# Two column tiles per transfer to the transposed adjacency, and list blocks of 128 columns instead of 124

## The chip, the cores and the metric

One core of a Trainium2 chip runs the whole kernel. The metric is device time in microseconds. The median of three runs before the change is 1015.22 us (1012.13 to 1015.25).

## What is computed

Four graph layers in sequence over 2708 nodes with 128 features each, in float32. `adj` is a 2708 x 2708 matrix, about 0.6% nonzero beside its diagonal; its pattern of nonzeros is symmetric, its values are not.

```python
def _L0_gnn_ref(X, H):                      # layer 0
    msg = jnp.matmul(H.T, X)
    inv_deg = 1.0 / H.sum(axis=0)
    inv_deg = jnp.where(jnp.isinf(inv_deg), 0.0, inv_deg)
    return msg * inv_deg[:, None]
...
messages = gelu(s[:, None, :] + d[None, :, :] + msg_b)     # layer 1, per nonzero
aggregated = jnp.einsum('ijd,ij->id', messages, adj)
...
agg = adj @ states                                         # layer 2, then a GRU cell
...
e = jnp.where(mask, leaky_relu(s_src[:, None] + s_dst[None, :]), NEG)   # layer 3, two heads
att = softmax(e, axis=1) @ h + x
```

Each layer starts with `h = max(layernorm(x), 0)` and ends with `x = x + layer(h, adj)`.

## The kernel before

Rows and columns are cut in tiles of 128 (`P`): 21 whole tiles and one of 20. Four tiles make a group, so there are six groups of rows (`s`) and six of columns (`c`); the last has two tiles, of 128 and 20.

**Layer 0** is a walk over cuts of `adj`: column group `c` outside, row group `s` inside (`order`, line 544). For each cut (`c`, `s`) it does four things at once.
- SyncE loads the cut, 512 columns and some more, into one of five buffers (`load_cut`, line 310, issue at line 320; `RING = 5`, line 286). The load of a cut two steps ahead is written in the program ahead of the step's own work (line 570). Cuts of the last column group (`z`) have buffers of their own and are loaded during the chunk `LAST - 2`, one a step (line 572).
- VectorE makes lists: for every row it takes the eight largest values of each block of `JB` columns and their places (`list_cut`, line 348: MAX8 at 360, the index search at 362). There are `NB` = 22 blocks. The blocks that hold the diagonal ("near" blocks) are first copied and cleared of it by GpSimd (`mask_near`, line 328: copy at 342, product at 343).
- TensorE turns the cut, tile by tile (transposes, line 406, into three buffers of PSUM), and multiplies it with `h` (line 392).
- ScalarE copies each turned column tile out of PSUM into a buffer `aT`, summing the degrees on the way (line 411), and sends it to `adjT` in HBM (`write_one`, line 366, issue at line 368). Layer 2 reads `adjT` much later (line 1388). One turn handles one column tile of four row tiles, 128 x 512 values or 256 KB; `aT` has six buffers. A write is issued one turn after its copy, so the ScalarE queue holds: copy, write of the turn before, one or two small steps of the layer norms (`next_steps`, `first_steps`), next copy.

All queues run in the order in which the program is written; `invert` (line 431) puts the first use of the summed degrees of a column group on VectorE, two steps into the next group (one step in the last).

The list blocks are `JB` = 124 wide, the tiles 128, so a cut must hold four list blocks and four tiles: its window (line 306) begins at 496 c and ends at 512 (c + 1), that is 512, 528, 544, 560 and 576 columns wide, and 228 for the last. Every row tile has two near blocks, the last tile one.

**Lists of the last rows.** Row tiles 17 to 20 (`LATER`) have their other blocks loaded and listed during layer 1, five a period (`late_blocks`, line 199; `load_late`, line 708; `list_late`, line 732); there are 80 of them. The last tile's are done by `load_wide` and `list_wide`.

**Layer 1** takes the listed entries per block (at most 128 of a block of 128 rows), gathers both ends with selection matrices, applies gelu and scatters. Its matrices per block have `width(b)` rows, up to `JB` (line 936). If a block holds more than 128 entries, or a row has eight in one block, a flag is set and a dense version of the whole computation runs (`check_lists`, line 1036).

The tile framework gives out the DMA semaphores: in the trace only eight numbers occur (101 to 108), which the DMAs of SyncE and ScalarE take in turn, in the order of the program.

Of the kernel before, what the change touches and what calls it, by code (L numbers as in the profile page):

```python
# [20 lines left out]
F32 = mybir.dt.float32  # L21
BF16 = mybir.dt.bfloat16
AF = mybir.ActivationFunctionType
ALU = mybir.AluOpType
# [6 lines left out]
P = 128  # L31
N = 2708
D = 128
NT = (N + P - 1) // P
FULL = N // P
TAIL = N - FULL * P
CH = 512
# [3 lines left out]
MASKED = -1e30  # L41
FMAX = 3.4028234663852886e38

JB = 124
NB = (N + JB - 1) // JB
S = 8
E = P
GROUPS = [(t, min(4, NT - t)) for t in range(0, NT, 4)]
# [3 lines left out]
def size(t):  # L52
    return min(P, N - t * P)


def width(b):
    return min(JB, N - b * JB)


@with_exitstack  # L60
def listed_layers(ctx: ExitStack, tc: tile.TileContext, x, adj, w, out, flag):
    nc = tc.nc
# [12 lines left out]
    adjT = dram.tile([P, NT, N], F32, name="adjT")  # L75
# [86 lines left out]
    degs = keep.tile([P, NT, len(GROUPS)], F32, name="degs")  # L162
# [27 lines left out]
    LATER = NT - 5  # L190
    AT_ONCE = 5
    EARLY = 2
    WIDE = 4

    def near_blocks(n):

        return range(n * P // JB, (n * P + size(n) - 1) // JB + 1)

    late_blocks = [(n, b) for n in range(LATER, NT - 1) for b in range(NB) if b not in near_blocks(n)]
    nc.gpsimd.memset(val[:, NT - 1, :, :], 0.0)  # L200
    nc.gpsimd.memset(col[:, NT - 1, :, :], 0.0)

# [82 lines left out]

    RING = 5
    BEHIND = 2
    WINDOW = CH + 16 * (len(GROUPS) - 2)
    l0, ending = ExitStack(), ExitStack()
    ordered = ExitStack()  # L290
    lastp = ending.enter_context(tc.tile_pool(name="l0z", bufs=1, side="right"))
# [1 line left out]
    once0 = l0.enter_context(tc.tile_pool(name="l0h", bufs=1))  # L293
    pool = l0.enter_context(tc.tile_pool(name="l0k", bufs=2))
    marked = l0.enter_context(tc.tile_pool(name="l0n", bufs=8))
    turned = l0.enter_context(tc.tile_pool(name="l0t", bufs=6))
    sump = l0.enter_context(tc.tile_pool(name="l0p", bufs=3, space=PSUM))
    turnp = l0.enter_context(tc.tile_pool(name="l0q", bufs=3, space=PSUM))
    h0 = once0.tile([P, NT, D], F32, name="h0")
# [5 lines left out]

    def window(c):

        return 4 * JB * c, min(CH * (c + 1), N)

    def load_cut(c, s):  # L310

        g0, gk = GROUPS[s]
        lo, hi = window(c)
        if c < LAST:
            a = rows_a.tile([P, 4, WINDOW], F32, name="a")
        else:
            a = lastp.tile([P, gk, hi - lo], F32, name=f"z{s}")
        cuts[c, s] = a
        if gk == 4 and (c, s) != (0, 0):
            nc.sync.dma_start(  # L320
                a[:, :, 0 : hi - lo], adj[g0 * P : (g0 + 4) * P, lo:hi].rearrange("(t p) e -> p t e", p=P)
            )
            return
        for n in range(g0, g0 + gk):
            m = size(n)
            nc.sync.dma_start(a[0:m, n - g0, 0 : hi - lo], adj[n * P : n * P + m, lo:hi])

    def mask_near(c, s):

        g0, gk = GROUPS[s]  # L330
        lo = window(c)[0]
        a = cuts[c, s]
        for n in range(g0, g0 + gk):
            m = size(n)
            for b in near_blocks(n):
                if b // 4 != c:
                    continue
                e, k = b * JB, width(b)
                e0, e1 = max(n * P, e), min(n * P + m, e + k)
                p = lastp if c == LAST else marked  # L340
                v = nears[n, b] = p.tile([P, JB], F32, name=f"near{n}_{b}" if c == LAST else "near")
                nc.gpsimd.tensor_copy(v[0:m, 0:k], a[0:m, n - g0, e - lo : e - lo + k])
                nc.gpsimd.tensor_tensor(
                    v[0:m, e0 - e : e1 - e], a[0:m, n - g0, e0 - lo : e1 - lo],
                    offdiag[0:m, e0 - n * P : e1 - n * P], ALU.mult,
                )

    def list_cut(c, s, n):

        m = size(n)  # L350
        lo = window(c)[0]
        units = []
        for b in range(4 * c, min(4 * c + 4, NB)):
            if b in near_blocks(n):
                units.append((b, nears.pop((n, b))[0:m, 0 : width(b)]))
            elif n < LATER:
                units.insert(0, (b, cuts[c, s][0:m, n - GROUPS[s][0], b * JB - lo : b * JB - lo + width(b)]))
        for k in range(0, len(units), 2):
            for b, v in units[k : k + 2]:
                nc.vector.max(val[0:m, n, b, :], v)  # L360
            for b, v in units[k : k + 2]:
                nc.vector.max_index(col[0:m, n, b, :], val[0:m, n, b, :], v)  # L362
# [7 lines left out]
    def work_cut(c, s, between=()):  # L370

        steps = iter(between)

        g0, gk = GROUPS[s]
        t0, tk = GROUPS[c]
        i0, iw = span(g0, gk)
        lo = window(c)[0]
        a = cuts[c, s]
        if s == 0:
            accs[c] = sump.tile([P, CH], F32, name="sums")  # L380

        dgs = []
        if c == s:
            for q in range(gk):
                m = size(g0 + q)
                e = (g0 + q) * P - lo
                dgs.append(marked.tile([P, P], F32, name="dg", bufs=4))
                nc.gpsimd.tensor_tensor(dgs[q][0:m, 0:m], a[0:m, q, e : e + m], ident[0:m, 0:m], ALU.mult)

        def products(n):  # L390
            m, w = size(n), span(t0, tk)[1]
            nc.tensor.matmul(  # L392
                accs[c][:, 0:w], h0[0:m, n, :], a[0:m, n - g0, t0 * P - lo : t0 * P - lo + w],
                start=(n == 0), stop=(n == NT - 1),
            )

        todo = list(range(g0, g0 + gk))
        js = list(range(t0, t0 + tk))
        turns = [js[q : q + 2] for q in range(0, tk, 2)] if gk < 4 == tk else [[j] for j in js]
        for js in turns:  # L400
            p = turnp.tile([P, CH], F32, name="p_T")
            k, n = size(js[0]), len(js)
            for i, j in enumerate(js):
                for q in range(gk):
                    m, e = size(g0 + q), j * P - lo
                    nc.tensor.transpose(  # L406
                        p[0:k, i * iw + q * P : i * iw + q * P + m], a[0:m, q, e : e + k], ident[0:m, 0:m]
                    )
            aT = turned.tile([P, CH], F32, name="aT")
            for i, j in enumerate(js):  # L410
                nc.scalar.activation(  # L411
                    aT[0:k, i * iw : (i + 1) * iw], p[0:k, i * iw : (i + 1) * iw], AF.Copy, accum_out=degs[0:k, j, s : s + 1]
                )
            write_one()
            written.append((
                adjT[0:k, js[0] : js[0] + n, i0 : i0 + iw], aT[0:k, 0 : n * iw].rearrange("p (j i) -> p j i", j=n)
            ))
            for _ in range(2 if c == 0 else 1):
                next(steps, None)
            if c > 0 and todo and gk == 4:  # L420
                products(todo.pop(0))
        for _ in steps:
            pass
        for n in todo:
            products(n)

        for q, dg in enumerate(dgs):
            m = size(g0 + q)
            nc.scalar.activation(dg[0:m, 0:m], dg[0:m, 0:m], AF.Copy, accum_out=own[0:m, g0 + q : g0 + q + 1])
# [1600 lines left out]
```

## Time and profile before

| | us |
|---|---|
| median of three runs | 1015.22 |
| the profiled execution | 1009.63 |
| its span, first to last instruction | 1007.8 |
| TensorE / VectorE / ScalarE / GpSimd busy in the span | 912.5 / 795.9 / 530.3 / 461.4 |
| layer 0, to TensorE's last product of it | 0 to 205.8 |
| lists closed, layer 1 begins | 206 to 250 |
| layer 1, then layers 2 and 3 | 250 on |
| `adjT` writes: 122, of which 105 of 256 KB | |
| loads of cuts: 24 whole groups (1024 to 1152 KB), some smaller | |
| late list loads in layer 1 | 21 |

All times below are from the profiled execution. A row of the waits says which engine and line stood idle, what released it, how long in total, how often, and the longest. A row of the windows gives, for a stretch, each engine's busy time and number of instructions, then the granted TensorE clock, the busy share of the DMA engines and the rate. A row of the timeline gives start, duration, engine, line and operation, and in brackets the idle time ahead of it and its releaser; "ACTq" and "SPq" are the issues of transfers from ScalarE's and SyncE's queues.

### The profile page before, as it was taken

The page shows a single profiled execution, that of the slowest core. Times are in us where ns is not written, and L with a number is a line of the kernel's source. Part 1 is how long each engine was busy: PE and PEld are TensorE (multiplying, and loading weights), DVE is VectorE, ACT ScalarE, POOL GpSimd, SP SyncE. Part 2 cuts the span into 40 slices and gives each one's busy share as a digit, 9 for nine tenths or more (in the row PEclk, how much of TensorE's full clock was granted, in tenths as well). Part 3 has the DMA queues.
Part 4 walks back from the last instruction along what each step waited for, and adds up shares of the span by engine and source line. Part 5 has one row for each costly group of instructions (what it writes and reads, how often), then busy time and mean ns, then how long its engine had stood idle before and what let it go on. Part 6 is the DMA issues. An engine that isn't in the chain of part 4 may idle for free. (4 is left out here: it accounts for less than half of the span.)

```text
span 1007.8 us, 22141 instructions
## 1 busy us (share of the span) xinstructions
PE 912.5 (91%) x7948; PEld 742.8 (74%) x7948; DVE 795.9 (79%) x2753; ACT 530.3 (53%) x1561; POOL 461.4 (46%) x588
## 2 busy tenths in 40 slices
PE   6799889945999999999999999999889999999983
PEld 3455455624999999999899744444678999999972
DVE  7999896976787898989966555676588977997793
ACT  5756557734666667667666324332322653564342
POOL 6413222424996779797966354443211300430142
PEclk9999999955999999999999899999899999999996
DMA  9999999422344334333322356654301574456000
GB/s 329 287 340 333 340 368 327 167 70 88 124 160 152 109 111 142 112 128 116 125 84 93 122 204 216 235 190 159 105 22 56 173 250 139 158 176 218 6 17 15
DMA packets 80458, 165.41 MB, mean 164 GB/s; under 512 B 9760, under 2 KB 25748, under 8 KB 80338
## 3 DMA queue, kind: packets, MB, share of 16 engines
q1 hardware_dynamic: 60358, 131.77, 39.7%
q10 hardware_dynamic: 19980, 32.14, 8.8%
q8 instruction: 64, 1.05, 0.4%
q14 instruction: 56, 0.46, 0.1%
HBM read 117.26 MB, written 30.87 MB: 147 GB/s over the span
## 5 line engine op out<-in xcount | busy, mean ns | idle before, releaser
L843 POOL TENSOR_SCALAR put<-count,line,value 128x128 f32<-128x128 f32 x176 | 199.7, 1146 | 10.9 <-PE agg L956 7.0
L1239 PE MATMUL att<-hv,wt 128*128 128x129 f32 x1672 | 196.0, 278 | 7.6 <-DVE wt L1209 6.2
L1239 PEld LDWEIGHTS att<-hv,wt 128*128 128x128 f32 x1672 | 192.2, 194 | 10.7 <-DVE wt L1209 8.7
L931 PE MATMUL p_m<-s,sel 128*128 128x128 bf16 x1452 | 162.3, 220 | 6.9 <-ACT g L943 4.6
L935 PE MATMUL p_m<-d,cols 124*128 124x128 bf16 (+1 forms) x1452 | 162.3, 220 | 3.9 <-DVE cols L874 3.9
L1209 DVE SCALAR_TENSOR_TENSOR wt<-row,lift,mask 128x1024 f32<-128x1024 f32 (+1 forms) x132 | 138.8, 1082 | 22.9 <-PE att L1239 22.9
L121 POOL TENSOR_TENSOR n_r<-n_r,minus_half 128x4 f32<-128x4 f32 (+1 forms) x28 | 39.6, 1413 | 243.5 <-DVE n_r L120 238.4
L956 PE MATMUL agg<-put,g 128*128 128x128 f32 (+1 forms) x968 | 123.5, 280 | 0.0
L392 PE MATMUL sums<-a,h 128*128 128x512 f32 x220 | 115.8, 622 | 1.6 <-ACT h L137 1.6
L956 PEld LDWEIGHTS agg<-put,g 128*128 128x128 f32 x968 | 114.2, 193 | 0.0
L406 PEld LDWEIGHTS p_T<-ident,a 128*128 128x128 f32 (+1 forms) x440 | 54.7, 144 | 77.1 <-issue 34.7
L931 PEld LDWEIGHTS <-sel 128*128 128x128 bf16 x1452 | 103.8, 98 | 8.6 <-issue 7.9
L1400 PE MATMUL p_agg<-a,hs 128*128 128x512 f32 (+2 forms) x264 | 107.7, 549 | 2.1 <-DMA a<-adjT 2.1
L935 PEld LDWEIGHTS <-cols 124*128 124x128 bf16 (+1 forms) x1452 | 102.8, 98 | 4.9 <-DVE cols L874 4.9
L943 ACT ACTIVATE g<-p_m 128x512 f32<-128x512 f32 x132 | 72.8, 553 | 59.4 <-PE agg L956 42.8
L852 ACT ACTIVATE put<-mine,value 128x128 f32<-128x128 bf16 x308 | 100.8, 393 | 0.0
L406 PE MATMUL p_T<-ident,a 128*128 128x128 f32 (+1 forms) x440 | 71.3, 283 | 24.6 <-ACT aT L411 18.0
L411 ACT ACTIVATE aT<-p_T 128x512 f32<-128x512 f32 (+2 forms) x132 | 71.0, 541 | 27.0 <-PE p_T L406 10.8
L1400 PEld LDWEIGHTS p_agg<-a,hs 128*128 128x128 f32 (+1 forms) x264 | 47.1, 191 | 49.2 <-issue 45.5
L362 DVE FIND_INDEX8 col<-val,a 128x8 uint16<-128x124 f32 x306 | 82.4, 281 | 0.0
L1362 ACT ACTIVATE hs<-hs 128x1354 f32<-128x1354 f32 (+1 forms) x44 | 58.4, 1329 | 39.5 <-DMA hs<-in_adj 39.1
L360 DVE MAX8 val<-a 128x8 f32<-128x124 f32 x306 | 70.9, 273 | 2.2 <-DMA a<-in_adj 2.2
(291 smaller groups left out, 1561.0 us busy)
## 6 DMA issues: line engine op xcount, KB each, us to landing
hs<-in_adj SPq DMA_DIRECT2D x42, 677.0 KB
adjT<-aT ACTq DMA_DIRECT2D x105, 256.0 KB
a<-adjT SPq DMA_DIRECT2D x20, 1280.0 KB
spread<-passed SPq DMA_DIRECT2D x22, 704.0 KB
later<-sel SPq DMA_DIRECT2D x22, 616.0 KB
a<-in_adj SPq DMA_DIRECT2D x5, 1152.0 KB
a<-in_adj SPq DMA_DIRECT2D x5, 1120.0 KB
a<-in_adj SPq DMA_DIRECT2D x5, 1088.0 KB
```

The lines of the kernel that those rows point to most:

```text
L362: nc.vector.max_index(col[0:m, n, b, :], val[0:m, n, b, :], v)
L392: nc.tensor.matmul(accs[c][:, 0:w], h0[0:m, n, :], a[0:m, n - g0, t0 * P - lo : t0 * P - lo + w], start=(n == 0), stop=(n == NT - 1),)
L406: nc.tensor.transpose(p[0:k, i * iw + q * P : i * iw + q * P + m], a[0:m, q, e : e + k], ident[0:m, 0:m])
L843: nc.gpsimd.tensor_scalar(st["put", 0][:, b, :], count, st["line"][:, b : b + 1], st["value"][:, b : b + 1], ALU.is_equal, ALU.mult,)
L852: nc.scalar.activation(st["put", 1][:, b - HP, :], st["mine"][:, b - HP, :], AF.Identity, scale=st["value"][:, b : b + 1])
L931: nc.tensor.matmul(p[:, b - b0, :], st["sel"][:, b, :], s3[:, q, t % 2, :], start=(q == 0), stop=False)
L935: nc.tensor.matmul(p[:, b - b0, :], st["cols"][0:kb, b, :], d3[0:kb, b, q, :], start=False, stop=(q == 2))
L943: nc.scalar.activation(g[:, 0:n, :], state[t].pop(("p", k))[:, 0:n, :], AF.Gelu)
L956: nc.tensor.matmul(agg, g[:, b - 4 * k, :], put, start=(b == 0), stop=False)
L1209: nc.vector.scalar_tensor_tensor(wt[:, 0:n], row[:, k, c : c + n], lift[:, j, k : k + 1], mask[:, j, c : c + n], op0=ALU.max, op1=ALU.mult,)
L1239: nc.tensor.matmul(banks[s // 3][:, s % 3, :], wt[:, q * P : (q + 1) * P], hv[:, j, k, :], start=(v < 2 and s // 3 not in touched), stop=( ...
L1400: nc.tensor.matmul(pa[:, 0:n], h[0:k, j, :], a[0:k, j - j0, 0:n], start=(j == 0), stop=(j == NT - 1))
```

## The change

List blocks become 128 wide (`JB = P`): still 22, of which the last is 20 wide instead of 104. Each row tile has one near block, exactly its diagonal tile, which GpSimd makes with one product instead of two copies and two products. The windows become 512 c to 512 (c + 1) with nothing extra, 148 for the last. Of the 84 blocks of row tiles 17 to 20 that aren't near, the first four (tile 17, blocks 0 to 3) are listed with cut (0, 4), so that 80 are left for layer 1. Column tiles go to `adjT` in pairs: `aT` has five buffers of twice the size, two turns fill one, and one transfer of 512 KB takes both. Where the row group is the last (148 rows), four column tiles go in one transfer; the last column group's tiles go one by one as before.

```diff
-JB = 124
+JB = P
...
-    late_blocks = [(n, b) for n in range(LATER, NT - 1) for b in range(NB) if b not in near_blocks(n)]
+    late_blocks = [(n, b) for n in range(LATER, NT - 1) for b in range(NB) if b != n]
+    late_blocks = late_blocks[len(late_blocks) % AT_ONCE :]
...
-    turned = l0.enter_context(tc.tile_pool(name="l0t", bufs=6))
+    turned = l0.enter_context(tc.tile_pool(name="l0t", bufs=5))
...
     def window(c):
-        return 4 * JB * c, min(CH * (c + 1), N)
+        return CH * c, min(CH * (c + 1), N)
...
-            a = rows_a.tile([P, 4, WINDOW], F32, name="a")
+            a = rows_a.tile([P, 4, CH], F32, name="a")
...
-        for n in range(g0, g0 + gk):
+        for n in range(g0, g0 + gk if c == s else g0):
             m = size(n)
-            for b in near_blocks(n):
...
-                nc.gpsimd.tensor_copy(v[0:m, 0:k], a[0:m, n - g0, e - lo : e - lo + k])
-                nc.gpsimd.tensor_tensor(
-                    v[0:m, e0 - e : e1 - e], a[0:m, n - g0, e0 - lo : e1 - lo],
-                    offdiag[0:m, e0 - n * P : e1 - n * P], ALU.mult,
-                )
+            p = lastp if c == LAST else marked
+            v = nears[n] = p.tile([P, JB], F32, name=f"near{n}" if c == LAST else "near")
+            nc.gpsimd.tensor_tensor(
+                v[0:m, 0:m], a[0:m, n - g0, n * P - lo : n * P - lo + m], offdiag[0:m, 0:m], ALU.mult
+            )
...
-            elif n < LATER:
+            elif (n, b) not in late_blocks and n < NT - 1:
...
-            aT = turned.tile([P, CH], F32, name="aT")
+            if not held:
+                aT = turned.tile([P, 2 * CH], F32, name="aT")
             for i, j in enumerate(js):
+                at = (len(held) + i) * iw
                 nc.scalar.activation(
-                    aT[0:k, i * iw : (i + 1) * iw], p[0:k, i * iw : (i + 1) * iw], AF.Copy, accum_out=degs[0:k, j, s : s + 1]
+                    aT[0:k, at : at + iw], p[0:k, i * iw : (i + 1) * iw], AF.Copy, accum_out=degs[0:k, j, s : s + 1]
                 )
             write_one()
-            written.append((
-                adjT[0:k, js[0] : js[0] + n, i0 : i0 + iw], aT[0:k, 0 : n * iw].rearrange("p (j i) -> p j i", j=n)
-            ))
+            held += js
+            if k < P or size(js[-1] + 1) < P or (len(held) + n) * iw > 2 * CH or js[-1] == t0 + tk - 1:
+                j, n = held[0], len(held)
+                written.append((
+                    adjT[0:k, j : j + n, i0 : i0 + iw], aT[0:k, 0 : n * iw].rearrange("p (j i) -> p j i", j=n)
+                ))
+                held = []
```

More of the change, by code (lines that the diff above doesn't have):

```diff
@@ L193, in listed_layers @@
     WIDE = 4
-    def near_blocks(n):
-        return range(n * P // JB, (n * P + size(n) - 1) // JB + 1)
-    late_blocks = [(n, b) for n in range(LATER, NT - 1) for b in range(NB) if b not in near_blocks(n)]
+    late_blocks = [(n, b) for n in range(LATER, NT - 1) for b in range(NB) if b != n]
+    late_blocks = late_blocks[len(late_blocks) % AT_ONCE :]
     nc.gpsimd.memset(val[:, NT - 1, :, :], 0.0)
@@ L287, in listed_layers @@
     BEHIND = 2
-    WINDOW = CH + 16 * (len(GROUPS) - 2)
     l0, ending = ExitStack(), ExitStack()
@@ L332, in mask_near @@
         a = cuts[c, s]
-        for n in range(g0, g0 + gk):
+        for n in range(g0, g0 + gk if c == s else g0):
             m = size(n)
-            for b in near_blocks(n):
[L336 to L341, printed above, removed]
-                nc.gpsimd.tensor_copy(v[0:m, 0:k], a[0:m, n - g0, e - lo : e - lo + k])
-                nc.gpsimd.tensor_tensor(
-                    v[0:m, e0 - e : e1 - e], a[0:m, n - g0, e0 - lo : e1 - lo],
-                    offdiag[0:m, e0 - n * P : e1 - n * P], ALU.mult,
-                )
+            p = lastp if c == LAST else marked
[3 more added lines that the diff above has]
+            )
     def list_cut(c, s, n):
@@ L353, in list_cut @@
         for b in range(4 * c, min(4 * c + 4, NB)):
-            if b in near_blocks(n):
-                units.append((b, nears.pop((n, b))[0:m, 0 : width(b)]))
-            elif n < LATER:
+            if b == n:
+                units.append((b, nears.pop(n)[0:m, 0:m]))
+            elif (n, b) not in late_blocks and n < NT - 1:
                 units.insert(0, (b, cuts[c, s][0:m, n - GROUPS[s][0], b * JB - lo : b * JB - lo + width(b)]))
@@ L408, in work_cut @@
                     )
-            aT = turned.tile([P, CH], F32, name="aT")
+            if not held:
+                aT = turned.tile([P, 2 * CH], F32, name="aT")
             for i, j in enumerate(js):
+                at = (len(held) + i) * iw
                 nc.scalar.activation(
-                    aT[0:k, i * iw : (i + 1) * iw], p[0:k, i * iw : (i + 1) * iw], AF.Copy, accum_out=degs[0:k, j, s : s + 1]
+                    aT[0:k, at : at + iw], p[0:k, i * iw : (i + 1) * iw], AF.Copy, accum_out=degs[0:k, j, s : s + 1]
                 )
             write_one()
-            written.append((
-                adjT[0:k, js[0] : js[0] + n, i0 : i0 + iw], aT[0:k, 0 : n * iw].rearrange("p (j i) -> p j i", j=n)
-            ))
+            held += js
[4 more added lines that the diff above has]
+                ))
+                held = []
             for _ in range(2 if c == 0 else 1):
```

## The prediction

> **What bounds the kernel now.** I read the windows first, cut at the borders of the stages, to see where the change can act.
>
> ```profile
> core 0: us, PE busy (x) PEld busy (x) DVE busy (x) ACT busy (x) POOL busy (x), PEclk, DMA share, GB/s
> 0.00:51.50 51.50, 36.51 (x138) 20.45 (x139) 45.76 (x298) 33.70 (x136) 28.00 (x90) 1.00 0.94 309
> 51.50:104.00 52.50, 49.21 (x231) 29.00 (x230) 52.29 (x348) 31.08 (x112) 10.66 (x32) 1.00 0.99 341
> 104.00:161.00 57.00, 49.24 (x210) 26.68 (x209) 42.80 (x284) 33.98 (x138) 16.54 (x42) 0.97 1.01 351
> 161.00:206.00 45.00, 43.20 (x232) 28.31 (x230) 40.20 (x260) 32.72 (x121) 15.49 (x45) 0.94 0.56 207
> 206.00:250.00 44.00, 19.29 (x138) 14.85 (x139) 31.86 (x95) 17.13 (x49) 13.95 (x19) 0.54 0.22 69
> ```
>
> Layer 0 fills the first four rows. VectorE is full from 51.5 to 104 (52.29 of 52.50). From 104 to 161 no compute engine is full, and from 161 to 206 TensorE is (43.20 of 45). The DMA engines show a share near 1 until 161. So something makes three engines wait in turn; the waits from 8 to 206 us say what.
>
> ```profile
> PE p_T L406 <- ACT aT L411: 18.0, 15, 2.3
> ...
> DVE inv_deg L435 <- ACT aT L411: 11.8, 2, 8.9
> ...
> ACT aT L411 <- DMA a<-in_adj: 8.5, 3, 3.8
> ...
> ACT junk L255 <- DMA a<-in_adj: 7.8, 3, 4.4
> ACT part_x L464 <- DMA a<-in_adj: 7.0, 2, 3.8
> ...
> ACT aT L411 <- DMA adjT<-aT: 5.7, 5, 3.2
> ...
> DVE val L360 <- DMA a<-in_adj: 2.2, 1, 2.2
> ```
>
> VectorE and TensorE wait for ScalarE's copies, and ScalarE for loads of cuts, though none of its instructions reads a cut: `part_x` and `junk` have nothing to do with one. With lines 265 and 152 (4.1 and 3.2) these waits are 30.6 us. The timeline shows how they come about.
>
> ```profile
> 101.80 0.20 ACT L411 ACTIVATION_READ_ACCUMULATOR aT<-p_T 128x1 f32 x1
> 105.46 0.33 ACTq L368 DMA_DIRECT2D adjT<-aT  x1
> 105.83 0.37 ACT L464 ACTIVATE part_x<-p_s,inv_deg 128x128 f32<-128x128 f32 x1 [3.84 <-DMA a<-in_adj]
> ```
>
> The write at 105.46 held ScalarE up, not `part_x`. Its operands name semaphore 107, last taken by the load issued at 95.34, which landed at 105.39 by the semaphore events. Eight numbers go round over both queues: an issue waits until the DMA eight places before it in the program has landed. A full step has now one load and four writes, so the third write of a step waits for the load of the *next* step; loads land 7.4 to 10.5 us after issue in this stretch.
>
> **What the skill says.** "DMA: Bandwidth & Descriptors", section "Why a DMA increments its semaphore by 16 and not by 1", asks for one semaphore per slot in flight, since two DMAs on one cannot be told apart; the trace agrees (each reuse follows the landing). The same page, "Queues, rings and completion order", has SP's and ACT's transfers on the same 16 engines, interleaved by packets; the trace agrees (both queues move bytes in the same windows), so a write can't starve a load, only share with it. "Rules for kernel authors" there asks for 1 MiB a DMA; 512 KB instead of 256 KB goes that way, but 256 KB writes that have the engines alone land in 2.0 us (174 to 190 us), so I count nothing for size.
>
> **The change, part by part.**
>
> *Writes in pairs.* 122 writes become 67: (5 x 5 x 2) + 5 + 12. A full step has three DMAs (one load, two writes), so eight places are 2.7 steps instead of 1.6. Eight before the second write of a step lies that same step's load, landed before its transposes began; the other write waits on a write. The 30.6 us of ScalarE stalls go; so does most of the 5.7 us for `aT` buffers (ten tiles of room, not six). 55 issues of 0.33 us (18 us of ScalarE's sequencer, mostly beside its copies) go too: hidden, counted at nothing; uncovered they would be a gain, the upper end.
>
> What is late next? I take three column groups, from TensorE's start on (1, 0) at 50.23 to (4, 0) at 158.31: 108.1 us.
> - TensorE alone: undisturbed turns start every 1.30 us, as here.
>
> ```profile
> 175.35 0.60 PE L406 MATMUL p_T<-ident,a 128*128 128x128 f32 x4
> 175.78 1.02 PE L392 MATMUL sums<-a,h 128*128 128x512 f32 x2
> 176.64 0.60 PE L406 MATMUL p_T<-ident,a 128*128 128x128 f32 x4
> ```
>
>   20 turns are 26.0 us, the short step (154.77 to 158.31) 3.5, turned sums and rows and `destinations` some 1.6: 31.1 a group, 93.4 for three. It could gain 14.7.
> - VectorE: it idles 2.9 + 2.2 + 8.9 = 14.0 there. It gets more work: MAX8 means 254 ns at 104 columns and 274 at 124, so 1 ns a column, and 4 columns on two searches over 3 x 68 blocks are +1.6. Before that, in group 0, +0.5 likewise and four blocks moved in (0.445 us each, from 0.89 a pair) +1.8; the first near wait (1.8) loses about 0.9 as one product replaces copies. It could gain 14.0 - 1.6 - 2.3 + 0.9 = 11.0.
> - DMA: windows shrink by 16 + 32 + 48 + 64 + 80 = 240 columns x 2708 rows x 4 B = 2.60 MB, about 212 columns or 2.30 MB of it in this stretch. At the present mean of 346 GB/s that is 6.6 us. If the rate rises as loads are no longer stopped and restarted (125 to 150 us shows 369), 37.4 - 2.3 = 35.1 MB take 95 us: 13.
>
> So the gain lies between 6.6 and 11.0, and with three resources this close no one reaches its limit; I take **8.5 us**. After 158.31 TensorE runs 47.5 us almost without idle whatever comes before, so what is gained passes to the end of layer 0 and no more is gained there. The last products end later than VectorE's lists (it waits 4.7 us at line 609), so its changes there count nothing: block 21 shrinks from 104 to 20 columns (84 ns x 2 x 18 = -3.0), the others widen. If TensorE were not the cover they would be within +-3.
>
> *Near blocks.* GpSimd loses 43 copies (288 ns) and 43 products (320 ns), 26 us, and gains 22 products at about 0.45, 10 us. GpSimd waits itself in layer 0 (57.8 us for `part_x` alone), so beyond the 0.9 above nothing.
>
> *Moved list blocks.* Tile 17's four blocks leave no DMA behind in layer 0 (the cut is there). In layer 1 80 blocks stay, but the slices of five shift: counted from the code, 21 load issues on SP become 25, of 0.36 to 0.49 us: +2 us of a queue that mostly waits, ahead of `later` and `passed` in it. Cost between 0 and +0.5; I take 0. Matrix products of 128 instead of 124 partitions stream the same 128 columns: 0. Layers 2 and 3 read `adjT` as before.
>
> **Sum.** 1009.63 - 8.5 = 1001.1 for a profiled execution; that one stood 5.6 below the median, so 1015.2 - 8.5 = **1006.7**.
>
> **The new wait.** A load's eighth predecessor becomes the second write of four steps before, issued by ScalarE about 5 us before the load's buffer comes free. SP stands at that wait, and all later loads queue behind it; TensorE and VectorE need them 22 us (four steps of 5.5) later. 256 KB writes land in 4 to 9 us now; if 512 KB need up to 10, the load leaves 5 us late and, at up to 10.5 to land, is 6 us early. I count 0.
>
> **The rivals.**
> - *Bandwidth is the bound.* The stalls pass from ScalarE to transposes waiting for cuts. For it: share 0.99 and 1.01. Against: in windows of 25 us the rate differs between 287 and 369 at shares of 0.92 to 1.05, and TensorE waits 0.2 us for loads after the start. Gain about 5: **1010**.
> - *Nothing comes of it.* VectorE is the pacer (full to 104), takes its +3.9 and waits for something else: **1014**. Against: its 14.0 idle all end on ScalarE or a load.
> - *Slower: the load waits for the big write.* If 512 KB writes took over 16 us to land, cuts arrive late; each us beyond, on 18 loads, is 18 us: at 17 us, 18 - 8.5: **1025**. Against: the room above.
> - *More than VectorE's limit*, with issues uncovered: gain 13, **1002**.
> - *Not what it says:* blocks of 128 could overflow their 128 slots and call the dense version. Counted from the reference's inputs the fullest has 125, the fullest row 6. Excluded.
>
> **Chances.** Main case 0.55; bandwidth 0.20; nothing 0.12; slower 0.08; more 0.05. Measurement tells 0.3% (3.0 us) from no change. Faster: 0.55 + 0.20 + 0.05 = 0.80; same 0.12; slower 0.08. The range 1002 to 1013.5 takes in the first two cases with their bounds and part of the third, leaving out at most 0.2.
>
> **What would show it.** Right: ScalarE's waits for loads at lines 464, 255, 265 and 411 fall from 30.6 to under 8; the wait at line 435 from 11.8 to under 4; TensorE begins (4, 0) at about 150 and ends layer 0 near 197; after that the traces run alike. Bandwidth: line 406 waits for `in_adj`. Slower: SP's waits end on `adjT<-aT`, and lists wait for cuts. Wrong altogether: a difference of over 3 us after 250.

## The result and the profile after

| | before | after |
|---|---|---|
| median of five runs, on one chip | 1012.8 us (1012.13 to 1015.25) | 999.5 us (996.87 to 1000.4) |
| the profiled execution | 1009.63 | 996.87 |
| its span | 1007.8 | 995.1 |

The ratio of the times is 0.9855, with an interval of 0.9835 to 0.9876. The medians lie 13.3 us apart, where 8.5 had been forecast. The forecast of 1006.7 stood on a median of 1015.2 for the kernel before; the five runs beside the changed kernel had 1012.8, so 2.4 of the 7.2 us missed are the base and 4.8 are the gain. The profiled executions, 12.8 apart, show where it lies. The starts and ends of instructions in the two traces give this (the first selection of rows, the `sel` comparison on VectorE, is where layer 1's chain begins):

| stretch | before | after | difference |
|---|---|---|---|
| start to TensorE's (1, 0) | 50.23 | 49.24 | -1.0 |
| (1, 0) to (4, 0), three column groups | 108.08 | 95.97 | -12.1 |
| (4, 0) to the first selection | 54.06 | 51.53 | -2.5 |
| first selection to layer 1's first product | 21.4 | 21.9 | +0.4 |
| layer 1's products, first to last | 330.1 | 331.6 | +1.6 |
| to layer 2's first product | 7.1 | 7.1 | 0.0 |
| from there to the end | 436.9 | 437.8 | +0.9 |

First the windows of the changed kernel, cut at the same four places as before (PE, PEld, DVE, ACT, POOL, then clock, DMA share, GB/s).

```profile
51.50:104.00 52.50, 52.50 (x249) 31.56 (x248) 52.29 (x347) 36.37 (x134) 8.60 (x19) 1.00 1.03 359
104.00:161.00 57.00, 55.45 (x264) 32.76 (x263) 56.79 (x374) 38.95 (x144) 13.59 (x29) 1.00 1.01 367
161.00:206.00 45.00, 32.49 (x191) 22.11 (x189) 37.41 (x222) 25.74 (x95) 12.25 (x29) 0.84 0.34 123
```

In the second row VectorE went from 42.80 to 56.79 of 57 us and TensorE from 49.24 to 55.45: the holes of the middle stretch are closed, and two engines are full at once. In the third, layer 0's last products are over at 189.15 (before 205.84).

The waits from 8 to 206 us of the changed kernel:

```profile
ACT aT L403 <- PE p_T L396: 23.8, 48, 2.7
...
PE p_T L396 <- ACT aT L403: 6.9, 6, 1.8
...
ACT sums_T L440 <- DMA a<-in_adj: 2.5, 1, 2.5
...
ACT junk L252 <- DMA z<-in_adj: 1.4, 1, 1.4
```

ScalarE's 30.6 us of waits for loads are 3.9, its 5.7 us for buffers are gone, and so is VectorE's wait for the degrees (11.8). TensorE waits 6.9 us for ScalarE's copies and not 18.0; instead ScalarE now waits 48 times, for 23.8 us, until TensorE has turned a tile (before 26 times, for 10.8 us). The order of who waits for whom has reversed. The timeline of ScalarE at the place shown before:

```profile
102.15 0.19 ACT L252 ACTIVATION_READ_ACCUMULATOR junk<-xs 128x1 f32 x1
105.65 0.62 ACT L245 CAST d<-d_r 128x512 bf16<-128x512 f32 x1 [3.31 <-DVE d_r L244]
105.77 0.37 ACTq L357 DMA_DIRECT2D adjT<-aT  x1
```

There is still a wait of 3.31 us, nearly as long as the 3.84 us that a load caused. But VectorE's subtraction ends it, and the write behind it is issued 0.12 us later without a wait of its own that shows.

### The profile page after: what moved, and what is told of

Read it like the earlier page. It is cut to its first block, busy times and chain, and to the rows that moved or that the text cites. A ratio compares the mean times of both kernels' runs of the same rounds, so it can differ in the third digit from the quotient of the medians.

```text
span 995.1 us, 21965 instructions
## 1 busy us (share of the span) xinstructions
PE 911.7 (92%) x7948; PEld 741.4 (75%) x7948; DVE 795.4 (80%) x2753; ACT 532.3 (53%) x1561; POOL 443.3 (45%) x524
## 3 DMA queue, kind: packets, MB, share of 16 engines
q8 instruction: 64, 1.05, 0.4%
## 5 line engine op out<-in xcount | busy, mean ns | idle before, releaser
L839 POOL TENSOR_SCALAR put<-count,line,value 128x128 f32<-128x128 f32 x176 | 196.2, 1125 | 11.7 <-DVE value L828 11.7
L931 PE MATMUL p_m<-d,cols 128*128 128x128 bf16 (+1 forms) x1452 | 161.8, 221 | 3.3 <-DVE cols L870 3.3
L381 PE MATMUL sums<-a,h 128*128 128x512 f32 x220 | 112.8, 608 | 1.6 <-ACT h L137 1.6
L931 PEld LDWEIGHTS <-cols 128*128 128x128 bf16 (+1 forms) x1452 | 101.6, 98 | 6.7 <-DVE cols L870 4.4
L351 DVE FIND_INDEX8 col<-val,a 128x8 uint16<-128x128 f32 x327 | 89.8, 287 | 0.0
L403 ACT ACTIVATE aT<-p_T 128x512 f32<-128x512 f32 (+2 forms) x132 | 71.3, 542 | 24.3 <-PE p_T L396 23.8
L396 PE MATMUL p_T<-ident,a 128*128 128x128 f32 (+1 forms) x440 | 70.3, 280 | 13.3 <-ACT aT L403 6.9
L349 DVE MAX8 val<-a 128x8 f32<-128x128 f32 x327 | 77.7, 279 | 0.0
```

The source lines that it names most:

```text
L381: nc.tensor.matmul(accs[c][:, 0:w], h0[0:m, n, :], a[0:m, n - g0, t0 * P - lo : t0 * P - lo + w], start=(n == 0), stop=(n == NT - 1),)
L396: nc.tensor.transpose(p[0:k, i * iw + q * P : i * iw + q * P + m], a[0:m, q, e : e + k], ident[0:m, 0:m])
L839: nc.gpsimd.tensor_scalar(st["put", 0][:, b, :], count, st["line"][:, b : b + 1], st["value"][:, b : b + 1], ALU.is_equal, ALU.mult,)
L931: nc.tensor.matmul(p[:, b - b0, :], st["cols"][0:kb, b, :], d3[0:kb, b, q, :], start=False, stop=(q == 2))
```

## The experiments

Kernels that share a value under "before beside it" ran on one chip, beside runs of the kernel before; that value is the median of those runs. "Groups" is TensorE's time from (1, 0) to (4, 0), "last part" from there to the first selection, each from one profiled execution.

| kernel | groups | last part | median | before beside it | ratio, interval |
|---|---|---|---|---|---|
| pairs only | 109.8 | 56.7 | 1015.86 | 1010.44 | 1.0049 [1.0029, 1.0070] |
| blocks only | 106.0 | 53.6 | 1007.71 | 1010.44 | 0.9971 [0.9955, 0.9987] |
| small writes between | 105.8 | 53.6 | 1009.74 | 1010.44 | 0.9993 [0.9975, 1.0012] |
| ten single buffers | 108.2 | 52.2 | 1007.61 | 1010.44 | 0.9967 [0.9942, 0.9991] |
| three double buffers | 108.8 | 56.5 | 1013.55 | 1009.82 | 1.0024 [1.0005, 1.0042] |
| four tiles a write | 95.0 | 59.5 | 1004.86 | 1009.82 | 0.9944 [0.9925, 0.9962] |
| before, sums after | 110.2 | 51.6 | 1010.47 | 1009.82 | 1.0007 [0.9991, 1.0023] |
| full last block | 95.9 | 51.6 | 994.38 | 1009.82 | 0.9853 [0.9832, 0.9874] |
| the changed kernel again | 95.9 | 51.5 | 995.94 | 1010.37 | 0.9875 [0.9838, 0.9911] |
| full last block again | 96.3 | 51.5 | 992.67 | 1010.37 | 0.9829 [0.9794, 0.9864] |
| half search | 95.6 | 51.3 | 996.52 | 1010.37 | 0.9860 [0.9814, 0.9906] |
| half search, before | 106.4 | 54.4 | 1006.62 | 1010.37 | 0.9968 [0.9950, 0.9986] |
| fewer products, half search | 91.6 | 46.9 | 991.71 | 1012.71 | 0.9807 [0.9770, 0.9844] |
| fewer products | 100.1 | 48.5 | 999.97 | 1012.71 | 0.9889 [0.9856, 0.9922] |
| before again | 107.5 | 56.4 | 1012.08 | 1012.71 | 0.9995 [0.9972, 1.0017] |
| before, sums after, again | 108.2 | 54.0 | 1009.81 | 1012.71 | 0.9975 [0.9953, 0.9997] |

The column of groups falls in two classes: 106 to 110 wherever one part of the change is missing, 95 to 96 where all of it is there. The two kernels that leave out products stand apart, and so does four tiles a write in its last part; both are taken up below.

### Which part does it?

**Theory:** the eight semaphores that the transfers take in turn stop ScalarE, and fewer transfers end that. **Rivals:** the gain is the smaller volume of the narrow windows, or the greater room in the buffers (ten tiles and not six).

*Pairs only.* The kernel before, writes in pairs as in the change, blocks of 124 and wide windows left. The windows' load buffers take 46 KB of a partition (5 x 4 x 576 x 4 B), so that only three double buffers find room.

```diff
-    turned = l0.enter_context(tc.tile_pool(name="l0t", bufs=6))
+    turned = l0.enter_context(tc.tile_pool(name="l0t", bufs=3))
...
-            aT = turned.tile([P, CH], F32, name="aT")
+            if not held:
+                aT = turned.tile([P, 2 * CH], F32, name="aT")
...
```

> Writes in pairs alone: blocks of 124 columns and the wide windows stay. Three double buffers, the same room of six tiles as before, since no more fits beside the wide windows. Theory (eight semaphores in turn: fewer transfers, so no transfer waits for a load still on its way): ScalarE's waits for loads fall from 30.6 us to under 8, VectorE's wait at the degrees from 11.8 to under 4, and the time is 1001 to 1005 us, most of the gain. Rival 1 (room: what counts is ten tiles of buffer instead of six): no gain, 1010 to 1014. Rival 2 (bytes: what counts is the 2.6 MB less): no gain, 1010 to 1014.

It is slower than before, where the theory had expected most of the gain. Its waits of ScalarE name no load at all any more; this row has taken their place:

```profile
ACT aT L414 <- DMA adjT<-aT: 47.7, 30, 4.3
```

The semaphores no longer stop ScalarE, but three double buffers do: the copy waits 30 times for a write that has not landed.

*Blocks only.* Blocks and windows as changed, writes one by one from six buffers.

```diff
-JB = 124
+JB = P
...
-        return 4 * JB * c, min(CH * (c + 1), N)
+        return CH * c, min(CH * (c + 1), N)
...
```

> Blocks of 128 columns and narrow windows alone: writes stay single, 256 KB, six buffers. Theory of the semaphores: ScalarE still waits for loads, 20 us or more; the time is 1008 to 1013. Rival 1 (room): 1008 to 1013 too. Rival 2 (bytes): most of the gain is here, 1001 to 1004.

It gains 0.3%. Narrower windows help a little, but ScalarE still waits 27.7 us for loads in five rows, of which two are:

```profile
ACT junk L252 <- DMA a<-in_adj: 6.6, 3, 4.1
...
ACT part_x L453 <- DMA a<-in_adj: 6.6, 2, 3.6
```

*Small writes between.* The changed kernel, with a write of 512 B to a scratch tensor at every turn that only half fills a pair. Room and volume stay as changed; a step has five transfers again.

```diff
                 held = []
+            else:
+                scrap = dram.tile([1, P], F32, name=f"scrap{c}_{s}_{js[0]}")
+                written.append((scrap, ident[0:1, :]))
```

> The changed kernel with one small extra write of 512 bytes to a scratch tensor on ScalarE's queue at each turn that only fills half a pair, so that the number of transfers a step, and with it the turn of the eight semaphores, is that of before, while sizes, buffers, bytes and blocks are those of after. Theory of the semaphores: the stalls come back, ScalarE waits for loads 20 us or more, VectorE waits at the degrees 8 us or more, and the time is 1006 to 1012. Rivals 1 and 2 (room, bytes): 999 to 1001, at most 1 us more for the extra issues.

The whole gain is gone, with half a kilobyte a time added. The waits for loads are back, 27.8 us in seven rows, at the same kinds of places:

```profile
ACT aT L403 <- DMA a<-in_adj: 9.9, 3, 4.6
...
ACT part_x L463 <- DMA a<-in_adj: 4.7, 2, 2.4
```

This isolates the number of transfers in the rotation: bytes, buffers and blocks are those of the changed kernel. That it is the rotation shows in the semaphore events too. All eleven of these waits stand behind the issue of a write whose semaphore was last taken by the SyncE load named as releaser, and the write goes out 0.02 to 0.08 us after that load's last landing; it is the same with all ten waits in the kernel before (0.08 us). What the experiment does not separate is the time of the added issues themselves: in the three groups there are 32 more of them, 8.3 us of ScalarE's queue, beside 23.0 us of waits for loads there.

*Ten single buffers.* The changed kernel, but each tile written alone from ten buffers of half the size.

```diff
-    turned = l0.enter_context(tc.tile_pool(name="l0t", bufs=5))
+    turned = l0.enter_context(tc.tile_pool(name="l0t", bufs=10))
...
```

> Blocks of 128 and narrow windows, single writes of 256 KB, but ten single buffers, the same room as five double ones. Theory of the semaphores: as with six buffers, less the waits for buffers (5.7 us of ScalarE before), so 1006 to 1012. Rival 1 (room): all of the gain, 998 to 1001.

The same room without the pairs leaves 26.8 us of waits for loads. Room alone is not it.

*Three double buffers.* The changed kernel with less room.

```diff
-    turned = l0.enter_context(tc.tile_pool(name="l0t", bufs=5))
+    turned = l0.enter_context(tc.tile_pool(name="l0t", bufs=3))
```

> The changed kernel with three double buffers for the turned column tiles in place of five; transfers, blocks and windows as changed. Theory (the rotation of the eight semaphores and the room in the buffers are both needed): ScalarE's waits for loads stay below 5 us, but it waits 20 to 50 us for a buffer whose write has not landed, VectorE's wait for the inverse degrees comes back (9 to 13 us), layer 0 ends 9 to 14 us later and the time is 1006 to 1012. Rival (fewer transfers in the rotation are enough, the 128-wide blocks having brought the rest): within 2 us of the changed kernel, 998 to 1001.5.

It is slower than the kernel before, and than the 1006 to 1012 of the theory. The waits are as the theory had them: no wait of ScalarE for a load, VectorE's wait for the degrees back at 11.0, and

```profile
ACT aT L403 <- DMA adjT<-aT: 41.8, 24, 4.2
```

These five together say that the gain needs two things at once, fewer transfers in the rotation and more room than three double buffers (five have it; four were not tried). The narrow windows are what makes room for them: load buffers of 512 columns take 41 KB of a partition instead of 46, and those of the last column group 13 KB instead of 20 (22 x 148 x 4 B, before 22 x 228 x 4 B).

*Four tiles a write.* The changed kernel with 1 MB a write and three buffers of four tiles.

```diff
-    turned = l0.enter_context(tc.tile_pool(name="l0t", bufs=5))
+    turned = l0.enter_context(tc.tile_pool(name="l0t", bufs=3))
...
-                aT = turned.tile([P, 2 * CH], F32, name="aT")
+                aT = turned.tile([P, 4 * CH], F32, name="aT")
...
-            if k < P or size(js[-1] + 1) < P or (len(held) + n) * iw > 2 * CH or js[-1] == t0 + tk - 1:
+            if k < P or size(js[-1] + 1) < P or (len(held) + n) * iw > 4 * CH or js[-1] == t0 + tk - 1:
```

> The changed kernel with four column tiles to a transfer (1 MB), three buffers of four tiles: one load and one write a step, two in the rotation. Theory (VectorE is at its limit in the three column groups, 0.2 us idle in 57, so fewer transfers bring nothing more): 998 to 1002; ScalarE waits up to 10 us for buffers in places where cover hides it. Rival A (each transfer saved still shortens layer 0): 993 to 997. Rival B (a write that starts two turns later and lands later empties the three buffers too slowly): buffer waits over 20 us and 1003 to 1010.

Rival B comes nearest, in its time: 1004.86. Its buffer waits were to be over 20 us, and are 18.0. The groups take 95.0, 1 us under the changed kernel, but the last part 59.5 and not 51.5. Of ScalarE's waits for buffers, 12.8 us lie behind 144 us. The rule of the Trainium skill that the forecast named, a megabyte a DMA ("DMA: Bandwidth & Descriptors", "Rules for kernel authors"), was no help here, where the buffer has to come free again: 512 KB from five buffers did better than 1 MB from three.

### What paces the groups now?

The changed kernel's VectorE is busy 95.66 of the 95.97 us of the three groups, so it looked like the bound. **Theory:** VectorE paces. **Rival:** TensorE or the transfers do.

*Half search*, on the changed kernel and on the kernel before: the position search looks at 64 columns only, and what lies in the other half is left out of the lists.

```diff
-                nc.vector.max_index(col[0:m, n, b, :], val[0:m, n, b, :], v)
+                nc.vector.max_index(col[0:m, n, b, :], val[0:m, n, b, :], v[:, 0 : min(64, width(b))])
```

> The changed kernel with the position searches of layer 0 over only the first 64 columns of each block (the positions in the other half are left out of the lists): 281 searches from the step (1, 0) on by 64 columns of 1 ns, 18 us of VectorE's 141.9 there. Theory (VectorE paces layer 0 after the change; TensorE's own limit of 93.4 us lies only 2.6 under the 96.0 that the three groups take): the groups take 93 to 95 us, the last lists end earlier, the first selection starts 4 to 9 us earlier, time 990 to 996. Rival (TensorE or the transfers pace it as well): 1 us or less, 997 to 1000.

> The kernel before with the same cut of its searches: 278 by 60 or 40 columns, 16.3 us of VectorE's 142.0. Theory (the stalls of ScalarE at the rotation pace two of the three groups): VectorE's idle time grows by most of it and the first selection starts 0 to 5 us earlier; 1007 to 1012. Rival (VectorE's work is what counts in the kernel before as well): 9 us or more, 1003 or less.

The theory falls. These are the sums over the three groups, the changed kernel first, the half search below:

```profile
sum 95.97, PE 94.42 PEld 54.80 DVE 95.66 ACT 64.15 POOL 20.27; mean PE 31.47 PEld 18.27 DVE 31.89 ACT 21.38 POOL 6.75
```

```profile
49.91:80.11 30.20, 30.20 (x138) 17.45 (x137) 27.00 (x208) 20.18 (x75) 3.72 (x9) 1.00 1.03 357
...
sum 95.61, PE 93.61 PEld 55.08 DVE 79.73 ACT 64.54 POOL 20.25; mean PE 31.20 PEld 18.36 DVE 26.58 ACT 21.51 POOL 6.75
```

VectorE has 15.9 us less to do (95.66 to 79.73), and the groups take 0.4 us less. The first group takes 30.20 us in both, with TensorE full: that is TensorE's own work, the same to the hundredth in the repeated run of the changed kernel. On the kernel before the cut gains 0.3% (1006.62, just under the 1007 to 1012 of its theory): there the stalls set the pace.

*Fewer products*, with the half search and without it: ten of a column group's twenty products of sums are left out, 0.87 us each.

```diff
         def products(n):
+            if n % 4 in (1, 2) and n < NT - 1:
+                return
```

> The changed kernel without ten of the twenty products of sums that a column group has (nodes 1 and 2 of every four tiles are left out of layer 0's sums), and with the position searches of layer 0 over 64 columns: TensorE has 8.7 us less a group (0.87 each), VectorE some 5 us less. Theory (TensorE's order of work paces the groups after the change): the three groups take 84 to 92 us where they take 96.0, until the transfers are the limit, and the first selection starts 5 to 13 us earlier; 983 to 993. Rival (the transfers pace the groups): the groups keep 95 to 97 us.

> The changed kernel without ten of the twenty products of a column group alone, VectorE's searches whole. If TensorE and VectorE stand at their limits together (VectorE was busy for 95.7 of 96.0 us in the groups), the groups take 94.5 to 96 us and the time stays within 1.5 us of the changed kernel; if TensorE alone paces, VectorE's 95.7 us being stretched by waiting, they fall to 84 to 92.

With both, the groups take 91.6, at the edge of the 84 to 92 of TensorE's theory. With TensorE's work alone cut they take 100.1, longer than with all of it. That was expected by neither. The third group and the sums with both cut, then the second group and the sums with the products alone:

```profile
102.56:140.36 37.80, 27.86 (x129) 16.86 (x129) 29.02 (x220) 23.52 (x93) 10.50 (x25) 0.91 1.05 376
sum 91.59, PE 77.38 PEld 48.21 DVE 80.71 ACT 63.44 POOL 20.89; mean PE 25.79 PEld 16.07 DVE 26.90 ACT 21.15 POOL 6.96
```

```profile
73.78:113.66 39.88, 27.29 (x129) 17.34 (x129) 39.78 (x262) 22.60 (x88) 9.54 (x24) 0.83 0.95 327
...
sum 100.13, PE 80.23 PEld 48.97 DVE 99.72 ACT 64.13 POOL 20.85; mean PE 26.75 PEld 16.32 DVE 33.24 ACT 21.38 POOL 6.95
```

In the second, VectorE is full (99.72 of 100.13) and the rest waits for it: ScalarE's `part_x` 7.8 us for the inverse degrees, and TensorE's transposes 19.1 for the copies queued behind. Two things belong to the 100.1. The stretch ends where TensorE starts (4, 0), and by then VectorE is seven searches further on than in the changed kernel (213 against 206), so that the last part is shorter in return: from (1, 0) to the first selection the two kernels take 148.6 and 147.5 us, with 142.4 and 141.9 of work for VectorE. And the granted clock, the third value from the end of a row, is 1.00 in all three groups of the changed kernel and 0.93, 0.83 and 0.84 here; what that adds is not separated. In time the two are not told apart: 0.9889 for fewer products and 0.9875 for the changed kernel again, with intervals that overlap.

Up to the first selection, less work for VectorE alone brings 0.6 us, less for TensorE alone nothing, less for both 9.0 (4.4 of them in the groups). So the two are at their limits together, within about a microsecond in 96. When both have less, the DMA engines show a share of 1.05 in all three groups at 376 to 390 GB/s; that the transfers are the next limit is read from this and was not tried by itself. Why the third group then takes 37.8, longer than with full work, stays open; the clock of 0.91 in its row is one candidate.

### The last part of layer 0

TensorE's last products end 47.5 us after (4, 0) before and 43.9 after. In the kernel before TensorE stands 1.5 us at `p_s`, where it turns the last column group's sums, for VectorE's copy `ends`, and the granted clock falls to 0.5 at 200.9 us, before the last products are done; after, that wait is 0.4 us and the clock falls at 191.2, 2 us behind them. **Theory:** this is the 2.5 us of the last part. **Rival:** the clock falls anyway, or the lists set the end.

*Before, sums after*, twice, the second time beside the kernel before itself:

```diff
         if (c, s) == (LAST - 1, LAST):
             turn_rows(LAST - 2)
             ranked = rank(0, FIRST, bank("p_r"))
-            turn_sums(LAST)
         work_cut(c, s, first_steps(s) if c == 0 else next_steps(c, s))
+        if (c, s) == (LAST - 1, LAST):
+            turn_sums(LAST)
```

> The kernel before, with the turning of the last column group's own sums queued after the step (4,5) on TensorE and not ahead of it, so that TensorE does not wait 1.5 us there for VectorE's ends. Theory (3.6 us of the gain at the end of layer 0 came from that wait and from the clock that fell to half behind it): the wait goes, the clock stays at 1.0 until the products end, these end 2 to 4 us earlier, and the time is 1007 to 1011 where the kernel before has 1012.8 (ratio 0.996 to 0.998). Rival (the clock falls whatever TensorE does there, or VectorE's last lists set the end of layer 0): the time is that of the kernel before within 0.1 per cent.

> The kernel before once more, for a second trace: from the start of the step (4, 0) to the first selection 53 to 55 us, with a wait of TensorE of over 1 us on VectorE's ends and a clock at 0.5 before the last products end. If the start of (4, 0) differs by 1 to 3 us from the 158.3 of the first trace, the groups ahead differ by chance between executions.

> The kernel before with the last column group's own sums turned after the step (4, 5), for a second trace beside that of the kernel before on the same chip. If the last part's gain is real: from the start of (4, 0) to the first selection again 51 to 52 us, and the time 1 to 3 us under the kernel before. If not: 53 to 55 us there, or a time within 1 us.

The second pair of traces shows the wait and the clock plainly, the wait and two windows of the kernel before first, the same with the sums moved below:

```profile
PE p_s L453 <- DVE ends L635: 1.8, 1, 1.8
```

```profile
202.00:204.00 2.00, 2.00 (x10) 1.46 (x9) 0.00 (x0) 1.05 (x7) 0.00 (x0) 0.85 0.02 6
204.00:206.00 2.00, 2.00 (x3) 0.50 (x2) 0.34 (x1) 1.07 (x5) 0.00 (x0) 0.50 0.49 152
```

```profile
202.00:204.00 2.00, 2.00 (x5) 0.48 (x6) 0.34 (x1) 1.07 (x6) 0.00 (x0) 1.00 0.47 148
```

With the sums moved the wait is gone and the clock is still 1.00 when the products end at 204.0; without, it is 0.50 and they end at 207.6. The last part is shorter by 2.5 us in the first pair (54.1 to 51.6) and by 2.3 in the second (56.4 to 54.0). The 54.0 lies where the expectation had it for no gain (53 to 55), but the kernel before has 56.4 beside it, 2.3 more than in its first trace. The first selection comes only 0.4 us sooner in the first pair and 1.7 in the second, since (4, 0) begins later with the sums moved. The times bear it out only half: 0.9975 with an interval below 1 in the second set, 1.0007 in the first, as the rival had it.

The clock mostly goes with the wait. Over all the traces it fell ahead of the last products' end where TensorE's wait at `p_s` was 1.4 us or longer (five traces), and behind it where the wait was under 0.5 us or absent (ten). Three do not fit: small writes between, where it fell at 200.3 us, 3.6 ahead of the end, after a wait of 0.4, and the two kernels with fewer products (0.4 and 0.7). That the change shortens the wait by the narrow block 21 on VectorE is argued only.

The Trainium skill has the clock fall after at least one idle window of about 3.4 us ("TensorE: Matmul & The Clock Gate", "What's actually happening"). Here waits of 1.5 and 1.8 us, shorter than such a window, came before it; no view shown here has the windows.

But the theory does not account for the 2.5 us. The first selection is VectorE's, so VectorE's own time says more. These are the sums from (1, 0) to the first selection, before and after:

```profile
sum 162.14, PE 146.11 PEld 87.30 DVE 142.02 ACT 99.46 POOL 45.11; mean PE 48.70 PEld 29.10 DVE 47.34 ACT 33.15 POOL 15.04
```

```profile
sum 147.50, PE 141.12 PEld 86.79 DVE 141.92 ACT 100.38 POOL 33.43; mean PE 35.28 PEld 21.70 DVE 35.48 ACT 25.09 POOL 8.36
```

VectorE works 142.0 us in the one and 141.9 in the other; its idle time fell from 20.1 to 5.6 us, and that is the gain of 14.6 us, groups and last part together. The second of its waits for the degrees, in the kernel before, lies across the border between the two:

```profile
160.35 0.18 DVE L435 TENSOR_REDUCE inv_deg<-degs 128x4 f32<-128x24 f32 x1 [8.90 <-ACT aT L411]
```

It ended 2.0 us after (4, 0) began at 158.31. So 2.0 of the 2.5 us are the end of the wait that the change removed in the groups. VectorE's later wait, at `d_r`, is for ScalarE's rounded copies `xb` of the listed values. Before, with the sums moved, and after the change it is:

```profile
DVE d_r L609 <- ACT xb L608: 4.7, 2, 4.0
```

```profile
DVE d_r L611 <- ACT xb L610: 2.2, 2, 1.6
```

```profile
DVE d_r L605 <- ACT xb L604: 4.4, 2, 3.7
```

Moving the sums saves VectorE 2.5 us here, the change 0.3: these are two different gains. The longer of these waits does end sooner after (4, 0) with the change, 43.5 us and not 45.2, or it would have grown; how much of that is TensorE's shorter wait and the clock is not separated.

### Where the 2 us in layer 1 come from

The four kernels with blocks of 128 that were traced first (the changed one, blocks only, small writes between, ten single buffers) took about 2 us more than the kernel before from the first product of tile 0 to that of tile 16 in layer 1 (243.2 to 243.3 against 241.4; pairs only, with blocks of 124, 240.8). It builds up tile by tile: those that took 13.41 and 14.27 us take 13.58 and 14.44. **Theory:** the last block. Its products run over 20 rows now and over 104 before. **Rival:** the 25 late loads. The ends of tile 5 on TensorE, before and after:

```profile
329.11 0.33 PE L931 MATMUL p_m<-s,sel 128*128 128x128 bf16 x3
329.28 0.33 PE L935 MATMUL p_m<-d,cols 104*128 104x128 bf16 x3
329.45 0.89 PE L956 MATMUL agg<-put,g 128*128 128x128 f32 x6
```

```profile
314.72 0.33 PE L927 MATMUL p_m<-s,sel 128*128 128x128 bf16 x3
314.98 0.34 PE L931 MATMUL p_m<-d,cols 20*128 20x128 bf16 x3
315.25 0.82 PE L952 MATMUL agg<-put,g 128*128 128x128 f32 x5
```

Three products start 0.17 us before the next row in the kernel before (55 ns each). After, 0.26 and 0.27 us pass: the first product of 20 rows starts 151 ns after its predecessor, the first product of `agg` 144 ns after the last of them, and the second another 213 instead of 164.

*Full last block.* The changed kernel with these products over 128 rows, 108 of them zero.

```diff
     d3 = fix.tile([P, NB, 3, D], BF16, name="d3")
+    nc.gpsimd.memset(d3[:, NB - 1, :, :], 0.0)
...
-                kb = width(b)
+                kb = JB
```

> The changed kernel with the last list block's three products in layer 1 taken over 128 rows, 108 of them zero, and not over the 20 that it has now (104 before the change). Theory (the loss in layer 1 comes from that short block: its first product starts 151 ns after the one before and not 56, the gather behind it comes 144 and 213 ns later and not 55 and 164; 0.23 us for each of 22 tiles): a tile takes 13.35 and 14.2 us where it takes 13.58 and 14.44, and the time falls by 4 to 5 us to 994.5 to 995.5. Rival (the loss comes from the 25 late loads with their cut slices, or from searches over 128 columns): the tiles keep their 13.58 and 14.44 us and the time is that of the changed kernel within 0.7 us.

```profile
314.24 0.33 PE L928 MATMUL p_m<-s,sel 128*128 128x128 bf16 x3
314.40 0.33 PE L932 MATMUL p_m<-d,cols 128*128 128x128 bf16 x3
314.57 0.89 PE L953 MATMUL agg<-put,g 128*128 128x128 f32 x6
```

The gaps are gone, and the tiles take 13.33 and 14.20 us, even less than before the change. Layer 1's products take 328.3 us from first to last where the changed kernel has 331.1 on that chip. The two side by side:

> The changed kernel once more, beside the same with a full last block on the same chip: 997 to 1000.5.

> The changed kernel with the last list block's products in layer 1 over 128 rows, beside the changed kernel on the same chip: 3 to 4.5 us below it (the tiles from 0 to 20 took 3.6 us less in its first profile), so 993 to 996.5; rival (layer 1's gain is given back behind it): within 1 us.

995.94 (under its 997 to 1000.5) and 992.67: 3.3 us. The intervals of the ratios, 0.9875 and 0.9829, overlap, but the slowest of the six runs with full rows, 993.92, is faster than the fastest of the six without, 994.81, and the tile times point to the same cause. The rival falls, since the late loads are the same. This is the fastest version that computes the whole result.

## Why the forecast was wrong

- **The mechanism was right.** The rotation of eight semaphores stopped ScalarE, pairs ended it: 30.6 us of waits became 3.9 (forecast under 8), the wait for the degrees 11.8 became nothing (under 4), (4, 0) begins at 145.2 (about 150). Small writes between and the semaphore events show it to be the cause. The condition that the forecast only mentioned in passing, "ten tiles of room, not six", is as necessary: with three double buffers the same pairs lose.
- **The step that failed** is the last one of the sum: "with three resources this close no one reaches its limit; I take **8.5 us**". The groups gained 12.1. TensorE's limit had been worked out as 14.7, VectorE's as 11.0, the transfers' as up to 13. Here engines that work from queues with buffers between them were full together: TensorE 94.42 and VectorE 95.66 of 95.97. There was no ground for a discount. Nor did the transfers hold it at their lower end, 6.6 us at 346 GB/s: they moved 360 GB/s in the groups of the changed kernel.
- **VectorE's limit was mis-sized too.** From its idle 14.0 us the forecast took off 1.6 for wider blocks and 2.3 for more work in group 0, and gave back 0.9. But group 0 lies ahead of (1, 0), where the stretch begins; for it 1.4 us of delay had been taken, and (1, 0) began 1.0 us earlier. And from (1, 0) to the first selection VectorE's work did not grow: 142.0 and 141.9 us. Its searches in block 21, which the forecast counted at nothing, took 5.8 us there and not 8.8; that is likely what offset the wider blocks. Against the 14.6 gained up to the first selection, the forecast's 8.5 lacks 2.5 of discount (11.0 to 8.5), 3.0 of deductions (14.0 to 11.0) and 0.6 of smaller waits.
- **"No more is gained there"**, after (4, 0), was wrong by 2.5 us in the profile. The 14.0 us were read as idle time "there", ahead of (4, 0), but the last 2.0 of them lie behind it. TensorE's 47.5 us, taken as the cover "whatever comes before", became 43.9: it had a wait of 1.5 us on VectorE and half a clock behind it. VectorE, whose "changes there count nothing", set the first selection with its waits.
- **"Matrix products of 128 instead of 124 partitions stream the same 128 columns: 0"** saw the wide blocks and not the last, which fell from 104 rows to 20. That cost 0.17 us in most tiles; with full rows layer 1's products take 2.8 us less and the kernel 3.3. "Wrong altogether: a difference of over 3 us after 250" came close: 1.6 in layer 1's products and 0.9 behind layer 2's start. The latter is not explained; it did not come back in the second trace (436.7 against 436.9).
- **The new wait** of a load for the write of four steps before came up once among the loads of cuts: SyncE stood 7.4 us for a write. It cost nothing that shows: the transposes wait 0.2 us for loads in all, as before.

The terms in sum, of the profiled executions: -1.0 - 12.1 - 2.5 + 0.4 + 1.6 + 0.0 + 0.9 = -12.7, which is the difference of the spans.

## What to carry to other kernels

When an engine waits for a transfer that its instruction never touches, look at the semaphore of the transfer it has to issue next: a fixed set given out in turn couples all queues, and the cure is fewer transfers in the turn, together with enough buffers to let the bigger ones land. Don't discount a gain because several resources are close to full; take the lowest limit that is worked out over the right stretch, one whose ends cut no wait in two, and check it by cutting the work of each alone and of both. When a size becomes round, look at what is left for the remainder.

## What the runs showed of the hardware

- Three products over 20 rows between products over 128 start about 95 ns late, and the next ones behind them some 89 and 49 ns late: 0.23 us a visit, in which zeros would have cost nothing. The Trainium skill says that a change of tiling mode drains TensorE ("TensorEngine Tiling (Array Packing)", "Key Properties"); the gaps agree with that, but no run here shows the mode. Products over 104 and 124 rows had no such gap.
- With ten of its products left out of each column group, TensorE was busy 80.2 of 100.1 us in the groups and was granted a clock of 0.93, 0.83 and 0.84; with all its work it was busy 94.4 of 96.0 us and had 1.00 throughout. From (1, 0) to the first selection nothing was gained (148.6 and 147.5 us).
- The clock fell to half 1.3 us after the end of a wait of 1.5 us, ahead of 4.9 us of work still to come.
